# Four stacked cross-attention layers: in the masked layers, two small steps of the softmax denominators get other due times

## The chip, the cores and the metric

The kernel runs on one core of one Trainium2 chip. The metric is the device time of one execution in microseconds; lower is better. The kernel before takes 4650.75 us, the median of 3 runs (4649.49 to 4656.12). Alongside these runs there is one execution taken with the hardware profiler. All durations below come from it.

## The reference

Four cross-attention layers run one after the other on `x` (1 x 2048 x 256, f32), with the same context `ctx_2048` (1 x 1601 x 512). Layers 0, 2 and 3 are "masked" layers with 16 heads of 64; layer 1 is a grouped layer with 16 query heads of 16 that share 4 key heads. A masked layer is, cut to what matters:

```python
q = hidden_states @ Wq                       # 2048 x 1024, 16 heads of 64
k = encoder_hidden_states @ Wk               # 1601 x 1024
v = encoder_hidden_states @ Wv
logits = jnp.einsum('bhqd,bhkd->bhqk', q, k) * scale
logits = logits + col_bias                   # -20 * (1 - mask) in the columns of 2 + 2 tokens
probs = jax.nn.softmax(logits, axis=-1)
out = jnp.einsum('bhqk,bhkd->bhqd', probs, v)
out = out.transpose(0, 2, 1, 3).reshape(B, HW, HEADS * HEAD_DIM)
out = out @ Wo + bo
out = out + residual
```

What this document turns on is the softmax's denominator: the sum of the exponentials over the 1601 keys, and the division by it.

## The kernel before, in words

**Units, steps and pairs.** A masked layer is worked through in 8 blocks of 2 heads, and a block in 4 units of 512 query rows. A unit goes over the keys in 13 chunks of 128 (the last has 65), one chunk a step. Scores stand transposed, keys on partitions and queries along the free axis, so that the exponentials can go straight into the product with the values. Three phases of different units overlap in each step: a chunk is scored (`masked_scores`, L715 on TensorE, then a copy to SBUF on ScalarE, L727, and a running maximum on VectorE, L732); a chunk of the unit before, 18 steps after it was scored, gets its maximum subtracted (VectorE, L806), is exponentiated (ScalarE, L811) and added to a running sum on GpSimd (L816, `sums`); and a chunk scored 20 steps before is multiplied with the values (TensorE, L851, `po`). The main loop takes two steps at a time, a *pair*: four score products, four value products, and what else is due. TensorE, VectorE and ScalarE execute in the order in which the program writes their instructions down.

**The end of a unit.** When its last value product is done, a unit still has four short steps ahead of it, and their due times are what the change touches. `add_up` (L884): two products of `sums` with ones add the sums over the partitions, ScalarE copies the result to the tile `by` (L888), and two small transfers on SyncE's queue bring it into columns (`den`, L893). `denominators` (L901): VectorE inverts those columns, one transfer writes them to DRAM (`cols<-rden`, L678) and two more spread them over all partitions into `by` (`by<-cols`, 128 KB each, L681). `divide` (L920): GpSimd multiplies the unit's output `oT` with `by`. `project` (L930): TensorE multiplies with Wo into a pair of score banks, and VectorE adds the result to the residual (L942).

**The maxima take the same road.** When a unit's 13 chunks are scored, TensorE transposes the running maxima (L775), VectorE reduces them (L776), one transfer writes them to DRAM (`cols<-ntop`, L678) and one of 512 KB spreads them over all partitions (`spread<-cols`, L681). ScalarE copies that into PSUM (L801) before the first subtraction of the next phase. All these transfers, and the loads of context slices (`ct`, 512 KB), of rows of x (`xT`, 512 KB) and of weights, stand in one queue, SyncE's, which issues in order: an issue that waits holds up those behind it.

**Due times and pieces.** What is not one of the three phases is a *piece* with a cost: the query projection of the next unit (L485), the four steps above, and *fill*, the projections of the next block's keys and values (L461, L415), of which a block has 14; the last ones of the keys and of the values are short, for the 65 last context rows. `finish()` of a unit returns its four pieces, each with the number of steps after the unit's last value product at which it is due. In each pair, `Pieces.pair` (L1109) first runs the pieces that are due, and then fill, but no fill if a piece that shares the spare PSUM bank `pm` (`add_up` does, `project` does not) has been run. Pieces come at the end of a pair. After a pair in which a piece took score banks (`project`) or in which the maxima were transposed they come at the front of the next pair instead (`front`, L1305), and such a pair has none at its end.

A unit has 13 steps, so that every second unit's last value product falls on the second step of a pair. These are called odd units here (the second and fourth of a block), the others even ones.

Of the kernel before, what the change touches and what calls it, by code (L numbers as in the profile page):

```python
# [26 lines left out]
Piece = namedtuple("Piece", "run cost shared", defaults=(True,))  # L27
# [7 lines left out]
def tile_cross_attention_stack(ctx: ExitStack, tc: tile.TileContext, t: dict, out: bass.AP):  # L35
# [648 lines left out]
    class Unit:  # L684
# [299 lines left out]
        def finish(self):  # L984

            if self.very_last:
                return [(0, Piece(lambda: self.quarters(of[len(units) - 2]), 2.0))]
            if self.final:

                at = 4 if self.b == NB - 2 else 2  # L990
                found = [
                    (at, Piece(self.add_up, 1.0)), (at + 2, Piece(self.denominators, 0.0)),
                    (at + 4, Piece(self.divide, 0.0)),
                ]
                if self.b < NB - 2:
                    found.append((10 - 2 * self.b, Piece(self.project_rows, 2.0, False)))
                return found
            if not self.masked:
                return [
                    (1, Piece(self.den_columns, 0.0)), (3, Piece(self.denominators, 0.0)),  # L1000
                    (6, Piece(self.divide, 0.0)), (8, Piece(self.project, 2.0, False)),
                ]

            at = 10 if self.u.n == self.layer.BLOCKS - 1 else 12
            return [
                (2, Piece(self.add_up, 1.0)), (4, Piece(self.denominators, 0.0)),
                (at - 4, Piece(self.divide, 0.0)), (at, Piece(self.project, 2.0, False)),
            ]

# [385 lines left out]
```

## Time and profile before

| what | value |
|---|---|
| median of 3 runs | 4650.75 us |
| the profiled execution, its own time | 4649.11 us |
| its span on the core | 4647.2 us |
| TensorE busy | 4529.5 us, 97% of the span |
| VectorE / ScalarE / GpSimd busy | 78% / 70% / 64% |
| share of TensorE in the chain that ended last | 90% |
| value products L851 / score products L715 | 1500.9 us / 1295.9 us busy |
| granted TensorE clock, mean | 0.987 |

The busy shares tell which engine has least to spare over the whole span. The chain that ended last follows back from the last instruction what released each instruction, so that its shares tell what the time is made of. Lines of a timeline give start and duration in us, the engine, the source line, the operation, what it writes and reads, the shapes and how many instructions are merged into the row; in brackets stands the engine's idle time before it and what ended that. A matrix product's end is modelled, so the difference of two starts is the better measure of what a group costs TensorE. SPq rows are issues on SyncE's queue, not transfers.

### The profile page before, as it was taken

How to read it: one execution, taken by the hardware profiler on the slowest of the kernel's cores; microseconds unless marked ns; L12 is line 12 of the kernel's file. 1: busy time of each engine (PE TensorE's matmuls, PEld its weight loads, DVE VectorE, ACT ScalarE, POOL GpSimd, SP SyncE). 2: the span in 40 equal slices, each digit the busy share in tenths (PEclk: the TensorE clock that was granted, in tenths of full speed). 3: DMA queues.
4: the chain of work that ended last, by engine and by line, in shares of the span. 5: the costliest groups of instructions: out<-in, count | busy, mean ns of one | idle time of the engine just before them, and what ended most of it. 6: DMA issues, size and time to landing. Idle time of an engine off the chain costs nothing.

```text
span 4647.2 us, 64011 instructions
## 1 busy us (share of the span) xinstructions
PE 4529.5 (97%) x23563; PEld 1853.4 (40%) x23563; DVE 3611.4 (78%) x3672; ACT 3263.8 (70%) x4108; POOL 2983.5 (64%) x1436
## 2 busy tenths in 40 slices
PE   8999999999899999999999999999999999999998
PEld 5444434443333333343344444344444444344432
DVE  5888888888766666652678888888888888888887
ACT  5777777777645555555667777777777777777776
POOL 3888888888620000000578887888888888878887
PEclk9999999999989999998899999999999999999999
DMA  5333333233201100021233333233232323332311
GB/s 160 85 90 82 87 81 88 78 86 84 71 24 34 28 22 22 20 62 31 70 91 82 88 82 87 77 88 85 77 94 82 92 82 87 81 88 78 85 38 39
DMA packets 377252, 338.01 MB, mean 73 GB/s; under 512 B 143781, under 2 KB 332741, under 8 KB 376940
## 3 DMA queue, kind: packets, MB, share of 16 engines
q1 hardware_dynamic: 373670, 328.54, 26.2%
q8 instruction: 186, 3.05, 0.3%
q0 software_dynamic: 1152, 3.28, 0.2%
q10 hardware_dynamic: 2118, 2.10, 0.1%
q14 instruction: 126, 1.03, 0.1%
HBM read 318.49 MB, written 14.69 MB: 72 GB/s over the span
## 4 chain that ended last, share of the span: by engine, by line
PE 90%; DVE 4%; ACT 2%; POOL 1%; issue 1%; DMA 1%; SPq 0%; ACTq 0%; DVEq 0%; POOLq 0%
PE po L851 28%; PE s L715 23%; PE t L746 9%; PE pm L415 6%; PE pm L461 6%; PE pm L485 4%; PE s L930 4%; DVE top L732 3%; PE s L775 2%; PE pm L884 2%; ACT p L727 2%; POOL sums L816 1%; PE t L821 1%; PE s L821 1%; PE pm L597 1%
## 5 line engine op out<-in xcount | busy, mean ns | idle before, releaser
L816 POOL TENSOR_TENSOR sums<-sums,p 128x1024 f32<-128x1024 f32 x1145 | 2714.9, 2371 | 627.3 <-ACT p L811 555.1
L732 DVE TENSOR_TENSOR top<-s,top 128x1024 f32<-128x1024 f32 (+1 forms) x1056 | 1290.8, 1222 | 344.6 <-ACT p L727 288.8
L851 PE MATMUL po<-p,v 128*64 128x512 f32 (+3 forms) x8320 | 1500.9, 526 | 6.4 <-ACT p L811 3.7
L806 DVE TENSOR_TENSOR p<-p,b 128x1024 f32<-128x1024 f32 (+1 forms) x1248 | 1478.2, 1208 | 1.9 <-ACT b L801 1.7
L727 ACT COPY p<-s 128x1024 f32<-128x1024 f32 (+1 forms) x1248 | 1224.0, 1015 | 336.2 <-PE s L715 276.8
L715 PE MATMUL s<-q,kT 64*128 64x512 f32 (+1 forms) x4992 | 1295.9, 625 | 43.8 <-DVE top L732 39.8
L811 ACT ACTIVATE p<-p 128x1024 f32<-128x1024 f32 (+1 forms) x1248 | 1264.6, 1058 | 39.5 <-DVE p L806 39.1
L851 PEld LDWEIGHTS po<-p,v 128*64 128x64 f32 (+3 forms) x8320 | 367.2, 125 | 1128.3 <-issue 989.1
L715 PEld LDWEIGHTS s<-q,kT 64*128 64x128 f32 (+1 forms) x4992 | 403.9, 182 | 756.3 <-DVE top L732 383.2
L833 ACT ACTIVATE p<-t 128x512 f32<-128x512 f32 (+1 forms) x760 | 413.9, 594 | 296.8 <-PE t L821 256.4
L759 DVE TENSOR_REDUCE row_top<-t 128x1 f32<-128x512 f32 x700 | 451.3, 687 | 199.1 <-PE t L821 166.5
L920 POOL TENSOR_TENSOR by<-oT,by 128x512 f32<-128x512 f32 x111 | 141.1, 1271 | 708.5 <-DMA by<-cols 521.6
L821 PE MATMUL t<-q,kT 32*128 32x512 f32 (+1 forms) x1520 | 489.6, 644 | 0.0
L746 PE MATMUL t<-kT,q 32*128 32x512 f32 (+1 forms) x1880 | 482.7, 553 | 0.0
L415 PEld LDWEIGHTS pm<-wv,ct 128*128 128x128 f32 (+1 forms) x2600 | 302.4, 187 | 89.2 <-issue 67.1
L415 PE MATMUL pm<-wv,ct 128*128 128x128 f32 (+2 forms) x2600 | 326.9, 278 | 2.2 <-ACT v L419 0.9
L461 PE MATMUL pm<-ct,wk 128*128 128x256 f32 (+1 forms) x1344 | 309.2, 373 | 3.6 <-DMA ct<-ctxT 2.1
L461 PEld LDWEIGHTS pm<-ct,wk 128*128 128x128 f32 x1344 | 233.3, 191 | 119.1 <-issue 83.2
L730 DVE TENSOR_TENSOR top<-s,p 128x1024 f32<-128x1024 f32 x96 | 117.6, 1225 | 202.8 <-ACT p L727 202.7
L746 PEld LDWEIGHTS t<-kT,q 32*128 32x128 f32 x1880 | 182.8, 185 | 164.1 <-issue 97.4
L776 DVE TENSOR_REDUCE ntop<-s 128x8 f32<-128x1024 f32 x96 | 117.6, 1225 | 123.7 <-PE s L775 123.7
L930 PE MATMUL s<-by,wo 128*128 128x512 f32 x376 | 187.8, 622 | 12.6 <-issue 6.9
(173 smaller groups left out, 2085.8 us busy)
## 6 DMA issues: line engine op xcount, KB each, us to landing
ct<-ctxT SPq DMA_DIRECT2D x288, 512.0 KB
xT<-xT SPq DMA_DIRECT2D x100, 512.0 KB
spread<-cols SPq DMA_DIRECT2D x96, 512.0 KB
by<-cols SPq DMA_DIRECT2D x190, 128.0 KB
xT<-xs SPq DMA_DIRECT2D x16, 512.0 KB
ct<-ctxT SPq DMA_DIRECT2D x48, 130.0 KB
wk<-in_L_xattn_Wk_dram SPq DMA_DIRECT2D x24, 256.0 KB
wv<-in_L_xattn_Wv_dram SPq DMA_DIRECT2D x24, 256.0 KB
```

Source lines behind the costliest of these rows:

```text
L415: nc.tensor.matmul(pv[:md, d, :f], ct(k)[:, d * P : d * P + md], wv[:, k, :], start=(k == 0), stop=(k == NCT - 1),)
L461: nc.tensor.matmul(pk, u.wk[:, k, :], ct(k), start=(k == 0), stop=(k == NCT - 1))
L715: nc.tensor.matmul(s[:m, h, :], self.u.kT[r, a : a + m], self.q[r, :], start=True, stop=(a != TAIL),)
L727: nc.scalar.copy(p[:m], s[:m])
L732: nc.vector.tensor_tensor(self.top[:m], s[:m], self.top[:m], ALU.max)
L746: nc.tensor.matmul(s[:, at : at + n], self.q[r, ts(q, P)], self.u.kT[r, a : a + n], start=True, stop=True,)
L759: nc.vector.tensor_reduce(self.top[:, of, q, k : k + 1], s, AX.X, ALU.max)
L806: nc.vector.tensor_tensor(self.p[c][:m], self.p[c][:m], self.less[:m], ALU.add)
L811: nc.scalar.activation(p[:m], p[:m], AF.Exp)
L816: nc.gpsimd.tensor_tensor(self.sums[:m], self.sums[:m], p[:m], ALU.add)
L821: nc.tensor.matmul(s[:m], self.u.kT[r, a : a + m], self.q[r, :], start=True, stop=True)
L851: nc.tensor.matmul(to, v, p, start=(c == 0 and not part), stop=(c == NT - 1 and part != 0))
```

## The change

In `finish()`, the first two of a masked unit's four pieces get other due times. `at` is 10 in a layer's last block and 12 in all others. So in seven blocks of eight `add_up` is due 3 instead of 2 steps after the unit's last value product, and `denominators` 5 instead of 4; in a last block it is 1 instead of 2, and 3 instead of 4. `divide` and `project` stay where they were. The last block of the last layer takes another branch and isn't touched.

```diff
             at = 10 if self.u.n == self.layer.BLOCKS - 1 else 12
             return [
-                (2, Piece(self.add_up, 1.0)), (4, Piece(self.denominators, 0.0)),
+                (at - 9, Piece(self.add_up, 1.0)), (at - 7, Piece(self.denominators, 0.0)),
                 (at - 4, Piece(self.divide, 0.0)), (at, Piece(self.project, 2.0, False)),
             ]
```

## The prediction

> **What bounds the kernel now.** I read the page first, for the engine with the least to spare, then the waits, then timelines of single units on each engine. The page:
>
> ```profile
> span 4647.2 us, 64011 instructions
> ...
> PE 90%; DVE 4%; ACT 2%; POOL 1%; issue 1%; DMA 1%; SPq 0%; ACTq 0%; DVEq 0%; POOLq 0%
> ```
>
> TensorE makes 90% of the chain that ended last, and it is busy 97% of the span. No work is added or taken away, so time can only come from how TensorE's groups follow each other, and can only be lost where TensorE is made to wait. This is an odd unit's projection and what follows it, on TensorE:
>
> ```profile
> 3010.01 1.98 PE L930 MATMUL s<-by,wo 128*128 128x512 f32 x4
> 3011.92 1.08 PE L884 MATMUL pm<-sums,ones 128*64 128x512 f32 x4
> 3012.93 1.99 PE L715 MATMUL s<-q,kT 64*128 64x512 f32 x8
> ...
> 3020.74 1.10 PE L461 MATMUL pm<-ct,wk 128*128 128x65 f32 x8
> 3021.78 1.99 PE L715 MATMUL s<-q,kT 64*128 64x512 f32 x8
> 3023.60 0.38 PE L722 MATMUL s<-bias_rows,tail_keys 64*65 64x512 bf16 x2
> ```
>
> The reader should see the projection, add_up right behind it, two bare pairs (3012.93 to 3020.74), then a fill piece of 65 columns. Starts differ by 1.91, 1.01, 7.81, 1.04 and 1.82: 13.59 us. The unit at 3456 has, by its place in a layer's last block, nearly the order that the change makes elsewhere:
>
> ```profile
> 3456.44 1.95 PE L930 MATMUL s<-by,wo 128*128 128x512 f32 x4 [0.44 <-issue]
> 3458.23 1.89 PE L461 MATMUL pm<-ct,wk 128*128 128x256 f32 x8
> ...
> 3465.99 1.94 PE L851 MATMUL po<-p,v 128*64 128x512 f32 x8
> 3467.76 1.03 PE L884 MATMUL pm<-sums,ones 128*64 128x512 f32 x4
> 3468.72 2.07 PE L715 MATMUL s<-q,kT 64*128 64x512 f32 x8
> 3470.72 1.94 PE L851 MATMUL po<-p,v 128*64 128x512 f32 x8
> ```
>
> Here a fill follows the projection: the projection takes 1.79 to the next start, not 1.91. The value products before add_up take 1.77, not the 1.87 they take before a fill; add_up takes 0.96, and the scores behind it 2.00 instead of 1.92. The last view is SyncE's queue with the maxima's road to ScalarE, and the worst case of that road, at another unit:
>
> ```profile
> 3026.77 1.12 SPq L681 DMA_DIRECT2D by<-cols  x2
> 3027.99 0.53 SPq L705 DMA_DIRECT2D xT<-xT  x1
> 3030.01 0.36 SPq L678 DMA_DIRECT2D cols<-ntop  x1
> 3034.09 0.33 SPq L681 DMA_DIRECT2D spread<-cols  x1
> ...
> 3038.97 1.02 ACT L801 COPY b<-spread 128x1024 f32<-128x1024 f32 x1 [0.64 <-DMA spread<-cols]
> ...
> 4168.00 1.02 ACT L801 COPY b<-spread 128x1024 f32<-128x1024 f32 x1 [1.61 <-DMA spread<-cols]
> ...
> 4172.54 1.96 PE L930 MATMUL s<-by,wo 128*128 128x512 f32 x4 [0.70 <-POOL sums L816]
> ```
>
> The maxima come just in time: ScalarE waited 0.64 us for them and TensorE paid nothing; it waited 1.61 and TensorE stood 0.70 us before the next projection.
>
> **What the change moves.** A pair holds two steps, so a step later means a pair later only where the due step was the last of its pair. Only odd units move: 42, by the order of the built programs. There add_up goes from the front of the pair behind the projection to the end of the pair after it, past sixteen score and sixteen value products, and a fill piece takes its place. In 38 of them exactly one fill is passed, nearly always the short 65-column one. So a short piece follows the projection still, of 1.04 us instead of 1.01. The 50 other units with this step keep their order, save 3 in last blocks where it goes forward by a pair at most; at up to 1 us each I leave them at 0 with bounds of plus and minus 3.
>
> **TensorE's order, on the path.** Before: 1.91 + 1.01 + 7.81 + 1.04 + 1.82 = 13.59. After, with the rows at 3456: projection 1.79 to 1.82 (the latter the median over the trace when a fill follows), fill 1.04, the two bare pairs with the last value products at 1.77 instead of 1.87, so 7.71, add_up 0.96, scores 1.82 + 0.08 = 1.90. Sum 13.40 to 13.43, a gain of 0.16 to 0.19 a unit. In 42 units it is 6.7 to 8.0 us; I take 7. Bounds: 3 (if the scores behind add_up wait 0.10 longer for VectorE's maxima, which end close to when they are wanted) and 10 (if they don't wait).
>
> **The reciprocal and its transfers.** In odd units the reciprocal (0.20 us on VectorE) comes a pair later, now right before the maxima's reduction, where VectorE stood idle 0.35 us waiting for the transposes: hidden. It needs the `den` transfers: add_up's start is 10.6 us after the projection's, ScalarE's copy ends 2 us later, the two issues take 1.14, and a small write on this queue lands about 3 us after its issue (3023.75 to 3026.77 for `cols<-rden`): 17 against 18.2 us, when VectorE gets there. It fits by a us; were it late by d, VectorE and all maxima would be late by d, at which the next paragraph's price holds. ScalarE's copy `by` (0.59) leaves a place where ScalarE waited 1.3 us for it and goes to one between exponentials and score copies that has 0.9 us of idle time: nothing.
>
> **SyncE's queue, the open term.** By the order of the built programs, the queue of an odd unit goes from "`by` twice, `xT`, `cols<-ntop`, `ct`, `spread`" to "`xT`, `cols<-rden`, `cols<-ntop`, `ct`, `by` twice, `spread`". So both `by` issues (1.12 us, waiting for `cols<-rden`) and their 256 KB stand straight before the maxima's transfer. No row of before shows that. Over 40 odd units with a full queue, the last packet of `spread` ends 7.96 us on average (standard deviation 0.68) after the issue of `cols<-ntop`. ScalarE is ready at 8.3 and sees the transfer 0.43 after its last packet. The projection comes 13.65 or 13.76 after that issue wherever ScalarE waits 0.91 or less, and then grows: waits of 0.94, 1.03, 1.19, 1.36 and 1.61 cost 0.09, 0.18, 0.29, 0.51 and 0.76. So TensorE pays what is beyond 8.72, in all 1.8 us now. Moved by 0.25, 0.5, 0.75, 1.0, 1.25 and 1.5 us, the same 40 arrivals would cost 3.5, 6.1, 10.7, 16.1, 23.3 and 31.7.
>
> How far do they move? Less than nothing is possible: `cols<-ntop` now lands 3.7 us after its issue in odd units, against 2.7 in even ones where no `xT` runs beside it, and `xT` would be done sooner without `by` before it; lower bound -0.5. The upper bound is all of `by`'s packets, which in the unit at 3010 ran from 3028.0 to 3029.75: +1.75, a cost of 41. Nearest is the slice `ct` of 512 KB that stands before `spread` already: with it `spread` ends 4.26 us after its issue, in the last block's units without it 3.9. So 512 KB issued 3.2 us ahead cost 0.4; 256 KB issued 1.1 us ahead, with 0.65 us left of 1.75 when `spread` begins, I put at 0.5. Cost 6.1 - 1.8 = 4.3 us.
>
> The Trainium skill speaks against the change here: DMA: Bandwidth & Descriptors, section "Queues, rings and completion order", says that each DMA engine consumes a queue's descriptors in ring order, and that a transfer's completion lands only after that engine's earlier writes. By that rule the whole +1.75 would count and the kernel would end 41 - 1.8 - 7 = 32 us later, at 4683. The row of `ct` before `spread` speaks for much less, and I go by it.
>
> **GpSimd.** The division keeps its place among the additions, and will wait for `by`. `by` landed 3.9 to 5.1 us after its second issue where GpSimd waited for it. With that issue about 3.1 after `cols<-ntop`, the division starts at 7.4 instead of 1.8, and the additions behind it 4 us later. ScalarE's score copies wait for them, since 22 probability tiles go round: the copy at 11.2 needs the first addition, which would end at 7.4 + 1.27 + 2.37 = 11.0; the copy at 12.2 the second, at 13.4. The second is 1.2 late, but what it feeds is wanted only after projection and fill, 3.6 us: nothing. Were the division later than 8.4 (7.55, and the 0.85 that ScalarE has), TensorE would pay.
>
> **Sum.** -7 + 4.3, rounded: -3 us. The profiled 4649.1 becomes 4646; it lay 1.6 below the median, so that the forecast for a median is 4648. About 0.2% (9.3 us) can be told from no change: no difference that can be measured.
>
> **Rivals.**
> (1) *`by` holds up the maxima, slower.* For it: the order of the queue, and that 18 of the 40 odd units have ScalarE waiting 0.3 us or more already. Against it: the transfers beside `xT` that go away. It decides from +1.05 us on (17.4 - 1.8 - 7 = +9). At 1.25 us: 23.3 - 1.8 - 7 = +15, 4665; at 1.5, +23, 4674.
> (2) *`by` lands late for GpSimd*, past 8.4 after `cols<-ntop`: each 0.5 us beyond costs up to 21 us over 42 units less the gain of 7, so 4665. For it: landings of 5.1 in the trace; against: the mean is 4.3.
> (3) *The order on TensorE pays in full and the maxima are no later*: -10 and -1.8, 4639. For it: lower bounds that the rows don't exclude; against: the scores' 2.00 behind add_up.
> (4) *The change does nothing*, since one short piece replaces another: 4651. Within the forecast's case, but the gaps 1.91 and 1.87 speak against it.
>
> **How the numbers follow.** Maxima later by -0.2 to +0.9, with the order's gain: 50%, 4642 to 4657 about 4648 (4 is in it). Rival 1: 30%. Rival 2: 6%. Rival 3: 14%. Range 4638 to 4674: from rival 3 to rival 1 at 1.5 us, some 10% left out on the slow side and few on the fast. Faster by over 0.2%: 15%; within: 49%; slower: 36%.
>
> **What would show it.** Right: after odd units' projections a 65-column fill at a start difference of 1.82, add_up 10.6 us after the projection with 1.77 before and 0.96 to the next start; VectorE without a wait for `den`; ScalarE's total wait for `spread` (13.7 us, 21 times) up to 20 to 35. Wrong: that total near 60 or more, with waits on TensorE before the projection (rival 1); ScalarE's score copies waiting for GpSimd's additions, and GpSimd for `by`, by 4 us and more a unit (rival 2); VectorE waiting for `den` and the maxima's write late. I would also be wrong if what TensorE gains at the projection is lost at its next wait for VectorE.

## The result

The changed kernel takes 4729.63 us, the median of 4 runs (4724.8 to 4738.57), beside 4651.29 us (4649.49 to 4656.12, 4 runs) of the kernel before on the same chip. The ratio is 1.0164, with a 95% interval of 1.0152 to 1.0177. The forecast was 4648 us in a range of 4638 to 4674: it missed by 82 us, in the direction of rivals 1 and 2, and beyond both. The profiled execution took 4732.87 us.

The page of the kernel after, with its span, and its chain by engine and by line:

```profile
span 4731.1 us, 63972 instructions
...
PE 78%; DVE 8%; issue 5%; DMA 4%; ACT 3%; POOL 1%; SPq 0%; another core or an unknown queue 0%; ACTq 0%; DVEq 0%; POOLq 0%
PE po L851 23%; PE s L715 19%; PE t L746 9%; PE pm L415 6%; PE pm L461 5%; DVE top L732 5%; PE s L930 4%; PE pm L485 3%; ACT p L727 2%; DMA cols<-rden 2%; DVE p L806 2%; PE s L775 2%; DMA spread<-cols 1%; POOL sums L816 1%; PE pm L884 1%
```

TensorE's share fell from 90% to 78%, and transfers rose from 1% to 4%: `cols<-rden` and `spread<-cols`, the two small roads through DRAM, are now on the chain by name. TensorE's busy time (4539.7 us) is 10 us more than before, the span 84 us more, so most of the loss is waiting.

First the part that went as forecast. This is a timeline of TensorE in the kernel after, from the projection to the tail scores of the moved order, the counterpart of the rows at 3010 of the kernel before (start, duration, engine, line, operation):

```profile
3058.59 1.98 PE L930 MATMUL s<-by,wo 128*128 128x512 f32 x4
3060.41 1.00 PE L461 MATMUL pm<-ct,wk 128*128 128x65 f32 x8
3061.35 1.99 PE L715 MATMUL s<-q,kT 64*128 64x512 f32 x8
...
3067.29 1.94 PE L851 MATMUL po<-p,v 128*64 128x512 f32 x8
3069.06 1.03 PE L884 MATMUL pm<-sums,ones 128*64 128x512 f32 x4
3070.02 2.01 PE L715 MATMUL s<-q,kT 64*128 64x512 f32 x8
3071.86 0.38 PE L722 MATMUL s<-bias_rows,tail_keys 64*65 64x512 bf16 x2
```

The 65-column fill stands behind the projection, `add_up` 10.5 us later, and nothing waits. From the projection's start to the tail scores it is 13.27 us; it was 13.59.

The loss is at the next projection. The same unit's transfers (SPq), then GpSimd, ScalarE, VectorE and TensorE, in the timeline of the kernel after; brackets hold the engine's idle time before the row:

```profile
3076.06 0.34 SPq L705 DMA_DIRECT2D xT<-xT  x1
3076.88 0.37 SPq L678 DMA_DIRECT2D cols<-rden  x1
3078.27 0.36 SPq L678 DMA_DIRECT2D cols<-ntop  x1
3078.80 0.55 SPq L264 DMA_DIRECT2D ct<-ctxT  x1
3083.08 1.12 SPq L681 DMA_DIRECT2D by<-cols  x2
3084.26 0.58 SPq L681 DMA_DIRECT2D spread<-cols  x1
...
3087.83 1.28 POOL L920 TENSOR_TENSOR by<-oT,by 128x512 f32<-128x512 f32 x1 [7.61 <-DMA spread<-cols]
3089.06 7.23 POOL L816 TENSOR_TENSOR sums<-sums,p 128x1024 f32<-128x1024 f32 x3
...
3089.01 1.02 ACT L801 COPY b<-spread 128x1024 f32<-128x1024 f32 x1 [2.41 <-DVE top L732]
...
3091.47 1.01 ACT L727 COPY p<-s 128x1024 f32<-128x1024 f32 x1 [0.20 <-POOL sums L816]
...
3092.51 1.23 DVE L732 TENSOR_TENSOR top<-s,top 128x1024 f32<-128x1024 f32 x1 [1.16 <-ACT p L727]
...
3093.84 1.96 PE L930 MATMUL s<-by,wo 128*128 128x512 f32 x4 [1.69 <-issue]
```

`spread` is issued 5.99 us after `cols<-ntop` (4.08 in the unit of before that the prediction shows), ScalarE stands 2.41 us before it can read it (0.64 before), GpSimd stands 7.61 us before its division, the score copy at 3091.47 waits for the first of GpSimd's additions behind it (three stand in the row, 2.41 us each), VectorE's maximum follows that copy, and the projection follows the maximum, 15.57 us after `cols<-ntop` instead of 13.76. The releaser that the trace names for ScalarE's 2.41 us is `top`, but the last packet of `spread` ended 10.34 us after `cols<-ntop`, and its last completion signal came at 10.66, 0.08 us before the copy began; I read that wait as one for `spread`. In the same way GpSimd's 7.61 us is a wait for `by`: the last signal of `by` came at 9.40, the division began at 9.56. The waits of the kernel after, over the whole execution (total, times, longest, in us):

```profile
ACT b L801 <- DMA spread<-cols: 93.2, 37, 5.1
ACT p L727 <- POOL sums L816: 61.4, 70, 1.4
...
PE s L930 <- issue: 51.2, 37, 2.1
...
PE po L851 <- ACT p L811: 13.9, 20, 2.6
PE s L930 <- POOL sums L816: 13.6, 11, 1.4
```

The first was 13.7 us in 21 waits before, the second 6.9 us in 8. TensorE's wait at the projection was 6.9 us under "issue" and 2.1 under GpSimd's additions.

**Two chains end at this projection.** I took the issue of `cols<-ntop` as zero in each of 37 odd units whose queue and neighbours are alike in all kernels. In the kernel before, TensorE paid what ScalarE waits for `spread` beyond 0.85 us: projection = 13.70 + (gap - 0.85). That is the maxima's chain. The other is GpSimd's: the division, one addition behind it, a score copy that needs the freed probability tile, VectorE's maximum of the same scores, and the projection; from the division's start it takes 6.0 us (1.23, 2.41, 1.04, 1.23 and 0.10 by the rows above). Both chains meet in that score copy, which ScalarE reaches, in its order, at the earliest 2.16 us after it begins to read `spread`. In all 37 units of the kernel after the projection starts 0.10 us after the end of that maximum. With the later of the two, the mean projection of the kernel after comes out at 15.77; it is at 15.78. GpSimd's chain is the later in 25 units, the maxima's in 12. Alone, the maxima's chain would cost these 37 units 65 us, GpSimd's 71, both together 77. The experiments take them apart. "Gap" below is the time from the end of ScalarE's instruction before to its reading of `spread` (a little below zero where the two overlap). "Late" is what all 37 projections together are beyond 13.70; the other columns are means over the same 37 units, in us.

| kernel | `spread` issued | its last packet | gap | division starts | projection | late in 37 units |
|---|---|---|---|---|---|---|
| before | 3.81 | 8.05 | 0.33 | 1.85 | 13.75 | 2 |
| after | 5.13 | 10.43 | 2.61 | 9.58 | 15.78 | 77 |
| denominators only | 4.97 | 10.00 | 2.19 | 9.21 | 15.35 | 61 |
| add_up only | 2.69 | 7.44 | -0.01 | 0.31 | 13.77 | 2 |
| division behind | 5.03 | 10.01 | 2.19 | 9.58 | 15.03 | 49 |
| by behind | 4.45 | 9.11 | 1.61 | 10.70 | 16.70 | 111 |
| both behind | 4.45 | 9.14 | 1.61 | 10.74 | 14.52 | 30 |
| without by (after) | 4.34 | 8.91 | 1.03 | not waiting | 14.06 | 13 |
| without by (before) | 2.63 | 7.19 | -0.03 | not waiting | 13.71 | 0.5 |
| all behind | 2.61 | 7.40 | -0.04 | 11.89 | 13.76 | 2 |

### The profile page after: what moved, and what is told of

Its sections match the earlier page's. It is cut to its first block, busy times and chain, and to the rows that moved or that the text cites. A ratio compares the mean times of both kernels' runs of the same rounds, so it can differ in the third digit from the quotient of the medians.

```text
span 4731.1 us, 63972 instructions
## 1 busy us (share of the span) xinstructions
PE 4539.7 (96%) x23563; PEld 1863.0 (39%) x23563; DVE 3617.0 (76%) x3672; ACT 3266.9 (69%) x4108; POOL 2981.5 (63%) x1436
## 3 DMA queue, kind: packets, MB, share of 16 engines
q14 instruction: 128, 1.04, 0.1%
## 4 chain that ended last, share of the span: by engine, by line
PE 78%; DVE 8%; issue 5%; DMA 4%; ACT 3%; POOL 1%; SPq 0%; another core or an unknown queue 0%; ACTq 0%; DVEq 0%; POOLq 0%
PE po L851 23%; PE s L715 19%; PE t L746 9%; PE pm L415 6%; PE pm L461 5%; DVE top L732 5%; PE s L930 4%; PE pm L485 3%; ACT p L727 2%; DMA cols<-rden 2%; DVE p L806 2%; PE s L775 2%; DMA spread<-cols 1%; POOL sums L816 1%; PE pm L884 1%
## 5 line engine op out<-in xcount | busy, mean ns | idle before, releaser
L930 PE MATMUL s<-by,wo 128*128 128x512 f32 x376 | 208.5, 682 | 68.3 <-issue 51.2
```

## The experiments

**Which of the two moved steps.** Denominators only (e1) has `add_up` where it was, and only the inversion later (the cuts of code show the edit against the changed kernel, where nothing else is said):

```diff
-                (at - 9, Piece(self.add_up, 1.0)), (at - 7, Piece(self.denominators, 0.0)),
+                (2, Piece(self.add_up, 1.0)), (at - 7, Piece(self.denominators, 0.0)),
```

> Only `denominators` gets its new due time; `add_up` stays where it was, so that TensorE keeps the order of the kernel before. Theory (the loss of 78 us is made by the late denominators' transfers, which hold up the maxima's transfer and the division): about 4737 us, 4715 to 4750, with the division starting 9 to 10 us after the maxima's column write in odd units and ScalarE waiting 80 to 110 us in all for `spread`. Rival (the new place of add_up on TensorE, in the spare PSUM bank and on ScalarE costs the time): 4651 us.

Measured 4727.34 us (4724.52 to 4728.85), 1.0173 times the 4649.5 us of the kernel before beside it (1.0149 to 1.0196). The later inversion alone makes the whole loss: the projection is at 15.35. TensorE's new order is not to blame.

Add_up only (e2) is the mirror of it:

```diff
-                (at - 9, Piece(self.add_up, 1.0)), (at - 7, Piece(self.denominators, 0.0)),
+                (at - 9, Piece(self.add_up, 1.0)), (4, Piece(self.denominators, 0.0)),
```

> Only `add_up` gets its new due time; the inversion keeps its place on VectorE, though its columns now come a pair later. Theory: the queue of transfers has the order of before again, with `by` ahead of the maxima, but VectorE stands some 2.5 to 3.5 us in each odd unit until the columns have landed, and the maxima with it: 4750 to 4790 us, with a wait of VectorE for `den` of over 80 us in all that before does not have. Rival (add_up's new place costs the time): 4730 us, without that wait.

Measured 4706.43 us (4705.64 to 4718.73), 1.0128 (1.0105 to 1.0151). Counted from `cols<-ntop` nothing is late and the projection is at 13.77, but VectorE runs into the inversion before its numbers are there, and `cols<-ntop` itself comes later. VectorE's waits in this run:

```profile
DVE rden L901 <- DMA den<-by: 73.5, 43, 3.9
```

The mechanism was as expected, with 73.5 us of waiting instead of over 80, its price 57 us and not 100 to 140. So the two steps can't be parted: the inversion must keep its distance to `add_up`, or VectorE, which works in order, stops for it.

**The two chains.** Division behind (e3) is the changed kernel, but in the odd units the division is put behind the addition of chunk 9, so that no addition waits for `by` while a probability tile is wanted:

```diff
+            latest["sum", c] = nc.cur_bb.bb.instructions[-1]
...
             nc.gpsimd.tensor_tensor(self.by, self.oT, self.by, ALU.mult)
+            if self.masked and not self.final and self.b % 2:
+                forced.append((nc.cur_bb.bb.instructions[-1], latest["sum", 9]))
...
-                (at - 4, Piece(self.divide, 0.0)), (at, Piece(self.project, 2.0, False)),
+                (at - 3, Piece(self.divide, 0.0)), (at, Piece(self.project, 2.0, False)),
...
+    for ins, behind in forced:
+        tc.add_manual_dep(ins, behind.name, order, reason="placed behind")
```

> The changed kernel, with the division of an odd unit held back on GpSimd behind two more additions (the tenth chunk's), so that its wait for `by` no longer holds up the additions that free probability tiles. Theory (two chains of nearly the same length reach the projection, one over the division and one over the maxima): only the second is left, 4651 - 7 + 70 = 4714 us (4700 to 4722), and ScalarE still waits some 95 us for `spread`. Rival a (the division alone is the cause): 4644. Rival b (the maxima alone): 4730.

Measured 4690.81 us (4683.55 to 4695.44), 1.0098 (1.0074 to 1.0123). ScalarE's waits for GpSimd's additions are gone, and what is left is the maxima's chain: by its gap of 2.19 the projection should start at 15.04, and it starts at 15.03. The time lies under the range that I had given: the gap itself shrank from 2.61 to 2.19, which the edit wasn't meant to do and for which I have no cause (denominators only, with the division in front, has 2.19 too).

By behind (e4) leaves the division in front of the additions, and issues the two `by` transfers of the odd units behind `spread`:

```diff
+        def spread_denominators(self):
+            if self.b % 2:
+                for h in range(2):
+                    src = self.rden_rows[slice(h, h + 1)].rearrange("(o h) p q -> o (h p q)", o=1)
+                    tile_ = self.by[self.rows(h)]
+                    nc.sync.dma_start(out=tile_, in_=src.to_broadcast(tile_.shape))
+                    forced.append((nc.cur_bb.bb.instructions[-1], latest["spread"]))
...
+                (at - 5, Piece(self.spread_denominators, 0.0)),
```

> The changed kernel, with the two `by` transfers of an odd unit placed behind the maxima's `spread` in SyncE's queue, and the division kept ahead of the additions where it was. Theory of two chains: the maxima are in time again (ScalarE waits under 20 us for `spread` in all), but the division starts 10 to 11.5 us after the maxima's column write and the projection 6.0 us after that, at 16 to 17.5 instead of 13.7: 4740 to 4800 us. Rival b (the maxima alone are the cause): 4644.

Measured 4810.39 us (4801.08 to 4818.94), 1.0353 (1.0324 to 1.0383). That is above the 4740 to 4800 that I had given. The waits of this run on ScalarE (the edits shift the line numbers):

```profile
ACT p L729 <- POOL sums L819: 152.5, 94, 3.4
ACT b L804 <- DMA spread<-cols: 55.7, 36, 3.3
```

GpSimd's chain explains the projection: 10.70 + 6.0 = 16.70, which is its mean. It doesn't explain all of the time: 111 us of lateness less a gain of 10 on TensorE would be 4750, and most of the other 60 us go with TensorE's granted clock (see the last section). And the second row is a miss. I had expected under 20 us there, and ScalarE still waits 1.61 us a unit for maxima that have no `by` in front of them any more. By the gap, less than half of the lateness of the maxima was `by`. Both behind (e5) joins the two edits:

> Both of the earlier treatments in the 2nd and 4th units: the two by transfers are issued behind spread, and GpSimd's division stands behind the addition of piece 9, so that nothing of GpSimd waits in front of a freed probability tile. Theory (two chains, and the maxima's own is late even without by in front of it, by ScalarE's 1.61 us gap that by-behind showed): the additions' wait at the score copies goes, the projection starts at 13.7 + (1.6 - 0.85) = 14.45 us after the issue of cols<-ntop, 0.75 us late in 37 units, 28 us; less the 7 us of TensorE's order: 4672 us (4660 to 4685). If the maxima were late only through the 256 KB of by, this run would give 4644 us.

Measured 4665.84 us (4660.77 to 4668.01), 1.0045 times the 4648.61 of the kernel before (1.0029 to 1.0062). With gap 1.61, unit by unit, the maxima's chain gives 14.52; the projection starts at 14.52. What is left of the lateness is real and is worth 30 us.

**What else holds the maxima.** Directly in front of `cols<-ntop` the change also put `cols<-rden`, 4 KB in pieces of 16 bytes. Without by (e6) and its counterpart with the schedule of before (e7) leave out the spreading of the inverted denominators, so that only this write is left in front:

```diff
             on_all_partitions(
                 rden,
+                [] if self.masked and not self.final else
                 [(self.by[self.rows(h)], slice(h, h + 1)) for h in range(len(self.pair))],
             )
```

> The changed kernel without the two transfers that spread the inverted denominators over the partitions, in masked units: the division reads what the tile by held before, so its wait is gone, and the queue loses 256 KB in front of the maxima; only the small write cols<-rden stays directly in front of cols<-ntop. What the time says is read against the kernel before with the same omission. Theory (the small write in front holds the maxima too): ScalarE still waits for spread, about 1.6 us in the 2nd and 4th units, and this run is some 20 us slower than its counterpart. Rival (only the bytes of by delay the maxima): no wait, and it is 7 us faster than its counterpart, by TensorE's order alone.

> The kernel before without the two transfers that spread the inverted denominators, in masked units (the division reads what the tile held before). In the kernel before these transfers were done before the maxima were written, and the projection was late by 2 us in all: both theories expect 4640 to 4651 us, the counterpart for the run without by of the changed kernel.

Measured 4638.47 us (4634.49 to 4646.2) for the changed schedule and 4638.67 (4634.51 to 4646.57) for that of before: equal, between the two expectations. The trace says why. SyncE's queue around one odd unit, first with the schedule of before, then with the changed one:

```profile
3020.42 0.33 SPq L705 DMA_DIRECT2D xT<-xT  x1
3022.64 0.36 SPq L678 DMA_DIRECT2D cols<-ntop  x1
3023.16 0.55 SPq L264 DMA_DIRECT2D ct<-ctxT  x1
3025.88 0.33 SPq L681 DMA_DIRECT2D spread<-cols  x1
```

```profile
3024.95 0.34 SPq L705 DMA_DIRECT2D xT<-xT  x1
3025.78 0.37 SPq L678 DMA_DIRECT2D cols<-rden  x1
3027.16 0.36 SPq L678 DMA_DIRECT2D cols<-ntop  x1
3027.69 0.55 SPq L264 DMA_DIRECT2D ct<-ctxT  x1
3032.05 0.33 SPq L681 DMA_DIRECT2D spread<-cols  x1
```

`spread` waits for the maxima's write to be complete: 3.24 us after its issue without the small write in front, 4.89 with it; over the 37 units 2.63 and 4.34. This delay of 1.7 us brings a gap of 1.03 on average, more in some units, and the units are late by 13 us in all, against 0.5. That eats TensorE's gain of 10, and the two kernels are equal.

All behind (e8) moves the small write as well: in the odd units the inversion stays where the change put it, but the write and both `by` issues come behind `spread`, and the division behind the addition of chunk 9. Against both behind:

```diff
-            self.rden_rows = dram.tile([4, P, QT], FP, name="cols", bufs=4)[:2]
-            with nc.allow_non_contiguous_dma(reason="1024 values, four at a time"):
-                nc.sync.dma_start(out=self.rden_rows.rearrange("h p q -> p h q"), in_=rden)
+            self.rden = rden
...
             if self.b % 2:
+                self.rden_rows = dram.tile([4, P, QT], FP, name="cols", bufs=4)[:2]
+                with nc.allow_non_contiguous_dma(reason="1024 values, four at a time"):
+                    nc.sync.dma_start(out=self.rden_rows.rearrange("h p q -> p h q"), in_=self.rden)
+                forced.append((nc.cur_bb.bb.instructions[-1], latest["spread"]))
```

> As with both behind, but in the 2nd and 4th units the small write cols<-rden is issued behind spread as well, so that nothing of the denominators stands in front of the maxima; the division stands behind the addition of piece 9. Theory (the small write in front delays the maxima): ScalarE's gap before it reads spread falls to about 0.3 us, as in the kernel before; by is issued some 3 us behind spread and lands about 12 us after cols<-ntop, the division ends near 13.3 and just about holds the projection at 13.7 to 14.1: 4644 to 4660 us. Rival (the maxima's transfers became slow through something else that the change moved, such as xT or ct): the gap stays at 1.6 us, and the time is 4670 us or more.

Measured 4638.58 us (4627.35 to 4643.58), 0.9976 times the kernel before (0.9965 to 0.9987). That is under the 4644 to 4660 that I had given, since the late division holds nothing up. `spread` is issued at 2.61, the gap is gone, and the projection is at 13.76, although the division starts only at 11.89. One unit in its timeline, SyncE, then GpSimd, then TensorE:

```profile
3022.01 0.36 SPq L678 DMA_DIRECT2D cols<-ntop  x1
3022.54 0.55 SPq L264 DMA_DIRECT2D ct<-ctxT  x1
3025.04 0.33 SPq L681 DMA_DIRECT2D spread<-cols  x1
3025.43 0.43 SPq L921 DMA_DIRECT2D cols<-rden  x1
3029.97 1.12 SPq L926 DMA_DIRECT2D by<-cols  x2
...
3033.46 1.28 POOL L940 TENSOR_TENSOR by<-oT,by 128x512 f32<-128x512 f32 x1 [1.94 <-DMA by<-cols]
...
3035.78 1.98 PE L952 MATMUL s<-by,wo 128*128 128x512 f32 x4
```

This settles where the loss of the change comes from: with the changed order on TensorE, and the inversion as late as the change has it, nothing is lost once the three transfers and the division stand elsewhere.

**Is it faster than before?** Before with all behind (e9) has the transfers and the division of all behind, but `add_up` at step 2 and so TensorE's order of before; all behind again (e11) ran beside it. The edit of e9, against all behind:

```diff
-                (at - 9, Piece(self.add_up, 1.0)), (at - 7, Piece(self.denominators, 0.0)),
+                (2, Piece(self.add_up, 1.0)), (at - 7, Piece(self.denominators, 0.0)),
```

> TensorE's order of the kernel before (denominators added up at step 2, the short piece behind the projection) with all-behind's order of transfers and division: inversion at step 5, the small write and the two by transfers behind spread in the 2nd and 4th units, the division behind the addition of piece 9. Against all-behind only TensorE's order differs, against the kernel before only the transfers and the division. Theory: TensorE's order is worth the 7 us that the prediction gave it (0.16 to 0.19 us in each of 42 units), and the maxima in time another 2 us against the kernel before: this run is 7 us (3 to 10) slower than all-behind, 4646 us when all-behind is at 4639. Rival: the order is worth nothing and all-behind's gain is the transfers': this run is equal to all-behind within 2 us.

> The kernel all-behind once more, beside its counterpart with the order of TensorE before and timed in five rounds: 4639 us, 0.15 to 0.35% under the kernel before.

Measured 4655.87 us (4650.42 to 4662.02) with the order of before, 1.0009 (1.0 to 1.0018), and 4651.0 us (4634.88 to 4656.69) for all behind, 0.9996 (0.9986 to 1.0006) of the 4650.89 of the kernel before. The order is worth 5 us by these medians, within the 3 to 10 expected, though the two intervals overlap. But all behind's lead over the kernel before is not repeated. I added up the 39 pairs of units that the change touches alike, from one issue of `cols<-ntop` to the next: 2922.2 us before, 2922.9 with all behind's transfers and the old order, 2912.3 and 2913.1 in the two runs of all behind, 3007.3 in the kernel after. So in these stretches the new order gains 9 to 10 us, in both runs. What lies outside of them, where the two programs are nearly the same, took 1724.8 us in the one profiled execution of all behind and 1736.2 in the other. At most 5 of these 11 us are time at half of TensorE's granted clock (126.9 us of it outside in the one, 136.1 in the other). In all behind again the clock and the time go together: ten of its eleven runs, at a mean granted clock of 0.984 to 0.986, took 4649.4 to 4656.7 us, and the one at 0.990 took 4634.9. That variation is as large as the gain, and I leave it open whether the whole kernel is faster than before by 0.2% or not.

**Is it SyncE's queue that makes the second small write late?** Other queue (e10) is without by, with `cols<-rden` issued by ScalarE:

```diff
-            nc.sync.dma_start(out=rows.rearrange("h p q -> p h q"), in_=cols)
+            (nc.sync if to else nc.scalar).dma_start(out=rows.rearrange("h p q -> p h q"), in_=cols)
```

> The run without by of the changed kernel (by is not spread in masked units, so the division reads old data), with one more edit: the small write cols<-rden is issued by ScalarE, on its queue, and not on SyncE's. In the run without by spread was issued 4.34 us after cols<-ntop, and 2.63 us with no such write in front. If the maxima's write waits in SyncE's ring behind the small write, spread's issue falls to 2.6 us (up to 3.0), ScalarE's wait for spread goes, and the time is 4632 us (6 us under the run without by). If the two writes meet behind the queues (in the DMA engines or in DRAM), spread is still issued at 4.0 to 4.4 us and the time stays at 4638 us.

Measured 4732.29 us (4727.49 to 4744.41), which neither side expected. Two rows of the timeline of ScalarE, and then TensorE's waits for the second of them over the whole execution:

```profile
3086.52 0.37 ACTq L678 DMA_DIRECT2D cols<-rden  x1
3086.93 0.60 ACT L488 ACTIVATE q<-pm 128x512 f32<-128x512 f32 x1 [2.05 <-PE s L775]
```

```profile
PE s L715 <- ACT q L488: 37.8, 46, 1.0
PE pm L415 <- ACT q L488: 20.4, 21, 1.0
PE pm L461 <- ACT q L488: 16.5, 17, 1.0
```

The issue stands in ScalarE's order in front of the copy of `q`, and TensorE waits 75 us for that copy; the time says nothing on the question. The transfers do: the small write is issued 1.38 us before `cols<-ntop`, as in e6, and `spread` is issued at 3.99 us, against 4.34 from one queue and 2.63 with no write in front. Most of the delay stays with two queues, so by this run most of it isn't made in SyncE's queue. Where the two writes meet behind the queues isn't told by it.

**The disputed cost by itself.** Extra write (e12) is the kernel before, in which the maxima of odd units are written twice:

```diff
                 self.spread = work.tile([P, 2, QB], FP, name="spread", bufs=1)
+                if self.b % 2:
+                    on_all_partitions(ntop, [])
```

> The kernel before with one thing added: in the 2nd and 4th units the small write of the maxima (4 KB) is done twice, into two different places, and only the second copy is spread. Nothing else moves: by is long on its way, TensorE's order is that of before. The second write is issued some 0.5 us later than the only one was. Theory (a small write directly in front holds up the completion of the next by 1.7 us, as 2.63 against 4.34 us without by says): spread is issued 1.5 to 1.9 us later after its write than in the kernel before (3.81 there), ScalarE's gap goes from 0.33 to about 2.3 us, and the projection is late by 1.4 us in 42 units: 4700 to 4725 us. Rival (the small write costs only its issue of 0.5 us): gap 0.8 us, 4650 to 4656 us.

Measured 4692.02 us (4681.66 to 4698.09), 1.0097 times 4647.35 (1.0072 to 1.0122). The second write comes 0.42 us after the first, and `spread` 4.89 after the second: 1.08 us later than the 3.81 of before, where I expected 1.5 to 1.9; the time is under the 4700 to 4725 that I had given. The gap is 1.93, and the projection comes 14.78 us after the first write; 13.70 + 1.93 - 0.85 is 14.78. So 4 KB alone, with nothing else moved, cost 45 us; the mechanism stands, its size depends on what else is under way.

## Why the prediction was wrong

**TensorE's order** was right and somewhat small. It was put at 0.16 to 0.19 us a unit, 7 us in all, with 10 as the upper bound. In the 39 pairs two units take 74.67 us on average in all behind, where nothing waits, instead of 74.93 before: 0.26, and 9 to 10 us in all. The projection's 1.82, the 1.77 and 0.96 around `add_up` were as forecast; the short fill takes 0.93 to 0.97 and not 1.04, and the scores behind `add_up` 1.85 and not 1.90.

**The inversion and `den`** were right: VectorE's waits for `den` are 4.4 us in all, against 3.9 before. That it fits by little is what add_up only shows from the other side.

**SyncE's queue, the open term,** is the step that failed. I put the shift of `spread`'s last packet at +0.5 us, between -0.5 and +1.75, for 4.3 us of cost. Measured, it moved from 8.05 to 10.43, by 2.4 us, above my upper bound, for 65 us. Two things were wrong in it. I priced the shift by the bytes in front of `spread`, `by` against `ct`, both of which are issued behind `cols<-ntop`: that comparison says nothing of `cols<-ntop` itself. So I moved only the second half of the maxima's road. The first half, from the issue of `cols<-ntop` to its completion, I held fixed or hoped to shorten, though the list of the new queue that I wrote down had the small write of `cols<-rden` directly in front of it. The runs make a ladder of `spread`'s last packet: 8.05 before; 7.40 with all three transfers behind it, so that the relief for which I had left -0.5 is there; 9.14 with the small write in front, +1.74; 10.01 with `by` in front too, +0.87 where I had put 0.5; and 10.43 in the kernel after. The last 0.42 stays open: the division stands in front of the additions there, but so it does in denominators only, at 10.00. The small write is the largest rung, and I hadn't priced it. I bounded the shift by bytes, and a transfer of 4 KB has next to none. The bound was read short besides: in the unit at 3010 the 128 packets of `by` run from 3028.09 to 3030.83, 2.74 us, and all but four of them end by 3029.85. The rule of the Trainium skill that I had set against the row (DMA: Bandwidth & Descriptors, "Queues, rings and completion order": ring order, and completion behind the engine's earlier writes) would have given 4683 by `by`'s bytes alone: nearer, and still 47 us too low.

**The price of lateness** was right. "TensorE pays what is beyond 8.72", read off five waits of the kernel before, gives the projection, unit by unit, to within 0.02 us on average in both behind, division behind, without by and extra write. What it has no term for is TensorE's granted clock, which falls around some of the late projections of the kernel after (the last section): some 24 us more.

**GpSimd** failed the same way: the division was to start at 7.4, with 8.4 as the point from which it costs; it starts at 9.58. The second `by` issue comes at 3.99 instead of 3.1, because it waits 4.8 us for `cols<-rden` and not 3, and the data take 5.6 us from there instead of 4.3. I let a term 1.0 us short of its own threshold go at nothing. Nor were 5.1 us the latest landing in the kernel before: in the masked layers GpSimd's waiting divisions start 3.0 to 5.5 us after the second issue, and 3.1 + 5.5 is past 8.4.

**The rivals.** Rival 1 (30%) and rival 2 (6%) both happened, and neither is the whole story: with GpSimd's chain away (division behind) the maxima's costs 49 us, and with the maxima's shortened (by behind) GpSimd's costs 111. Both go back to two small writes standing close together, `cols<-rden`, for which `by` waits, and `cols<-ntop`, for which `spread` waits, so they weren't independent, and I had priced them as if one excluded the other. The range ended at 1.5 us for rival 1 and at 4665 for rival 2, and the measured lateness is past both.

## What to carry to other kernels

When a change puts a small transfer in front of another one on a latency path, count the completion of the small write too, not its bytes: here 4 KB in pieces of 16 bytes cost the next write 1.1 to 1.7 us, more than the 0.9 us of the 256 KB of `by` behind it. Price every chain that ends at the same instruction, and before putting one at zero because it misses its threshold by a microsecond, ask what the other moved steps do to its transfers. A step that is due later takes its transfers with it: the arithmetic can move while the transfers are issued behind the urgent ones, and only then does the gain of the order show.

## What the runs showed that I had not expected

The packets of the 16-byte writes themselves are not slow. In the first odd units, the last one of the maxima's write ends 1.1 us after its issue both with the schedule of before and with the changed one, without `by` (256 packets in the one, 512 in the other); on average at 1.40 and 1.48. But the issue that waits for them comes at 2.63 and 4.34. The trace also has the 16 completion signals of each transfer: the last one of the maxima's write comes at 2.59 and 4.31 on average. So the completion comes 1.2 us after the last packet in the one and 2.8 in the other, where two such writes are close together. What it waits for isn't shown by any run here.

Behind such a write the large transfers start late as well. In the odd units of the kernel after, `ct` is issued 0.54 us after `cols<-ntop`, and in the trace of the packets hardly anything moves from 1.5 to 3.5 us; `ct`'s packets begin only then (behind the maxima's write alone, in all behind, from about 3). So the 512 KB of `ct` meet `by` (6 to 8.5 us) and `spread` (7 to 10 us), which before they had partly left behind by then (`ct` from 2.5 to 6).

Taking a transfer away can leave the time equal: without `by`, the two schedules take 4638.5 and 4638.7 us, because a gain of 10 us on one engine and a loss of 13 us on another path cancel. The equal medians alone would have looked like a change that does nothing.

Lateness has a second price, in TensorE's granted clock. In 13 of the 39 pairs of the kernel after the profile shows the clock at half for 3.4 or 6.8 us around the late projection; here it is at half from 2623.6 to 2627.0:

```profile
2623.12 3.25 PE L930 MATMUL s<-by,wo 128*128 128x512 f32 x4 [1.77 <-issue]
2626.16 2.38 PE L415 MATMUL pm<-wv,ct 128*128 128x128 f32 x16
```

The same two groups take 1.96 and 1.95 us in the unit at 3093.84. Over the 39 pairs this is 54.6 us at half the clock in the kernel after and 112.6 in by behind, 13.7 in denominators only, 6.8 in extra write, and none in before, both behind, division behind and all behind. It fits the times: the pairs of the kernel after are 95 us longer than those of all behind, of which the later projections are 71; in by behind it is 157 and 105. The remaining 24 and 52 us are a little under half of the time at half the clock. That the waits bring the lower clock about is suggested by where it falls, and not tested on its own.
